# Starting layer one with its first Strassen product instead of the router's projection, and running its seven products in another order

## The chip, the core and the metric

The kernel runs on one core of a Trainium2 chip. A core has a matrix engine (TensorE, PE in the profile, with its weight loads shown apart as PEld), a vector engine (VectorE, DVE), a scalar engine (ScalarE, ACT), GpSimd (POOL), and SyncE (SP), which here issues nearly all transfers. Each engine takes its own instructions strictly in the order in which they were written down; engines meet only at semaphores. The metric is the time of one execution on the device in microseconds (us); lower is better.

## The reference, cut to what matters

Two layers run one after the other, each adding to `x` (8 sequences of 256 tokens, 1024 channels, float32 throughout).

```python
# layer one: dense weight W plus a mixture of 8 rank-16 adapters, 2 of 8 chosen per token
base   = einsum('btd,od->bto', x, W)
logits = einsum('btd,ed->bte', x, Wr) + one_hot(language_ids) * 5.0
topw, topi = top_k(logits, 2);  weights = softmax(topw)
gates  = sum(one_hot(topi) * weights)               # 8 per token
h      = einsum('btd,erd->bter', x, A)              # 8 x 16 per token
x = x + base + 2.0 * einsum('bter,bte,eor->bto', h, gates, B)
# layer two: one whole 1024 x 1024 weight per sequence, chosen by adapter id
x = x + einsum('bsi,boi->bso', x, weight[adapter_ids])
```

`language_ids` and `adapter_ids` are two lists of eight integers.

## The kernel before, in words

**Blocks.** In layer one `x`, `W` and the result are cut into 2 x 2 blocks (`xb`, `yb`, `wb`, keys "11", "12", "21", "22"; the first digit of an `xb` key is the half of the channels, the second the half of the tokens). With the identity added to the diagonal blocks of `W` (`add_identity`), `x + base` is one matrix product, and it is done with seven block products instead of eight (Strassen-Winograd). Inside each of the seven, `product` does the same once more: seven inner products on quarter blocks, so that a block product is seven groups of four 128x512 matmuls. It accumulates in PSUM banks named `A`, `B` and `X`, and its four result quarters are copied out by ScalarE (`evict` without a base) or added up by VectorE (`evict` with one). The sums and differences that an inner product takes as operands (`s1`, `t1`, `s2`, `t2`, `s3`, `t3`) are made by VectorE in `make_subs`; `late` makes two more in the middle of a product. Block-level sums come from `x_sum` and `w_sum`.

**Router.** `project(j, c)` multiplies a quarter of the tokens (half `j`, half of that `c`, 512 tokens) with `Wr` and all `A` together (136 columns, `aw_sb`, kept in block `y12` until that is needed): 32 matmuls over eight blocks `k` of 128 channels. VectorE then adds the language bias to the logits (`lg`), and ScalarE copies the adapter part out (`hT`). `gating(j)` is a chain of some twenty small VectorE operations (with one exponential on ScalarE in it) that finds the two largest logits and their weights, and ends with `onto_h`, which scales `hT` by the gates. `turn(j)` transposes `hT` on TensorE (`ps_g`) and copies it to `hg`. Four of the seven block products (2, 5, 3 and 4) take the adapters' part along: they get `lora` and `tokens`, and `mm` then adds two matmuls with `hg` to a group. The language ids reach all partitions through a small matmul with ones (`use_ids`); `use_adapter_ids` makes the adapter ids that layer two's loads read.

**Order.** From `manual_schedule` on, every engine's order is the order of the calls. VectorE's spare work is put in a list, `todo`, with a cost in us and a first place at which it may run; `pump(place)` after each inner product takes its share off that list. TensorE goes through: ten matmuls on the identity that only warm it up (`WARM`), `project(0, 0)`, `project(0, 1)`, `project(1, 0)`, `project(1, 1)`, `turn(0)`, and then the products 1 (with `turn(1)` behind it), 2, 5, 3, 6, 7, 4, and layer two's eight sequences (`adapt`).

**Transfers.** All 1-MB loads of `x` and `W` are issued by SP in the order of need; the first three pieces for the router's weights `awT` and the two lists of ids are issued by ScalarE. Eight completion semaphores go round, so a load waits until the load eight places earlier has landed. Layer two's weights (`load_w1`) overwrite blocks of `x` and `W` that are no longer needed, so each of these loads waits for the last reader of its block.

Of the kernel before, what the change touches and what calls it, by code (L numbers as in the profile page):

```python
# [16 lines left out]
P = 128  # L17
# [4 lines left out]
WARM = 10  # L22
# [3 lines left out]
def kernel(  # L26
# [25 lines left out]
    nc = tc.nc  # L52
# [30 lines left out]
    def flat(blk):  # L83
        return blk.rearrange("p k n -> p (k n)")

    def bank(name):
        return psum.tile([P, 2, TQ], F32, name=name, tag="acc")
# [8 lines left out]


    aw_sb = flat(yb["12"])[:, : KC * EA].rearrange("p (k e) -> p k e", k=KC)
    hT = [flat(yb["22"])[:, j * C * ER : (j + 1) * C * ER].rearrange("p (c e) -> p c e", c=C) for j in range(2)]
    b_sb = const.tile([ER, O], F32, name="b_sb")  # L100
    ids = const.tile([1, 2, NB], I32, name="ids")

    def load_x(queue, i, j, c, k0, k1):
        queue.dma_start(  # L104
            xb[f"{i+1}{j+1}"][:, k0:k1, c * TQ : (c + 1) * TQ], xT[i, j, c, :, k0:k1, :]
        )

    def load_w(i, j):
        nc.sync.dma_start(wb[f"{i+1}{j+1}"], wT[i, j])

    def load_aw(queue, k0, k1):
        queue.dma_start(aw_sb[:, k0:k1, :], awT[:, k0:k1, :])

    load_aw(nc.scalar, 0, 1)
    load_x(nc.sync, 0, 0, 0, 0, 1)
    load_aw(nc.scalar, 1, 3)
    load_x(nc.sync, 0, 0, 0, 1, 2)
    load_aw(nc.scalar, 3, 8)
    load_x(nc.sync, 0, 0, 0, 2, 4)
    load_x(nc.sync, 1, 0, 0, 0, 2)  # L120
    load_x(nc.sync, 1, 0, 0, 2, 4)
    load_x(nc.sync, 0, 0, 1, 0, 4)
    nc.scalar.dma_start(ids[:, 0, :], lang)
    nc.scalar.dma_start(ids[:, 1, :], adapt)
    load_x(nc.sync, 1, 0, 1, 0, 4)
    load_x(nc.sync, 0, 1, 0, 0, 4)
    load_x(nc.sync, 1, 1, 0, 0, 4)
    load_w(0, 0)
    load_x(nc.sync, 0, 1, 1, 0, 4)
    load_x(nc.sync, 1, 1, 1, 0, 4)  # L130
    nc.sync.dma_start(b_sb, bT)
# [12 lines left out]
    nc.vector.tensor_copy(desc, desc_i)  # L144
    ecol = const.tile([P, E], F32, name="ecol")
    nc.vector.tensor_copy(ecol, ecol_i)
    ids_f = const.tile([1, 2 * NB], F32, name="ids_f")
    bias = const.tile([P, NB, E], F32, name="bias")
    aid_i = const.tile([1, NB], I32, name="aid_i")
    ones = const.tile([1, P], F32, name="ones")  # L150
    nc.vector.memset(ones, 1.0)

    def use_ids():
        nc.vector.tensor_copy(ids_f, ids.rearrange("o t b -> o (t b)"))
        wide = bank("ids_wide")[:, 0, :NB]
        nc.tensor.matmul(wide, lhsT=ones, rhs=ids_f[:, :NB], start=True, stop=True)  # L156

        nc.vector.tensor_tensor(
            bias,
            wide.unsqueeze(2).to_broadcast([P, NB, E]),  # L160
            ecol.unsqueeze(1).to_broadcast([P, NB, E]),
            ALU.is_equal,
        )
        nc.vector.tensor_scalar(bias, bias, LANG_BIAS, None, ALU.mult)

    def use_adapter_ids():

        wrap = const.tile([1, NB], F32, name="wrap")
        nc.vector.tensor_scalar(wrap, ids_f[:, NB:], 0.0, float(NAD), ALU.is_lt, ALU.mult)
        nc.vector.tensor_tensor(wrap, ids_f[:, NB:], wrap, ALU.add)  # L170
        nc.vector.tensor_scalar(aid_i, wrap, 0.0, float(NAD - 1), ALU.max, ALU.min)
# [4 lines left out]
    def add(out_, x, y):  # L176
        tt(out_, x, y, ALU.add)
# [1 line left out]
    def minus(out_, x, y):  # L179
        tt(out_, x, y, ALU.subtract)  # L180

    def add_identity(blk):

        d = bass.AP(blk.tensor, blk.offset, [blk.ap[0], [OG + P, KH], [1, P]])
        add(d, d, ident.unsqueeze(1).to_broadcast([P, KH, P]))


    hg = [const.tile([ER, 2, TQ], F32, name=f"hg{j}") for j in range(2)]
    lg = [rpool.tile([P, C, E], F32, name=f"lg_{j}", tag=f"lg{j}") for j in range(2)]
    gate8 = {}  # L190

    def project(j, c):

        ps = bank(f"ps_h_{j}_{c}")
        for k in range(KC):
            for r in range(CQ):
                v, u = divmod(r, 2)
                nc.tensor.matmul(  # L198
                    ps[:, v, u * EA : (u + 1) * EA],
                    lhsT=xk(k, j, c)[:, ts(r, P)],  # L200
                    rhs=aw_sb[:, k, :],
                    start=(k == 0 and u == 0),
                    stop=(k == KC - 1),
                    skip_group_check=True,
                )
        if (j, c) == (0, 0):
            use_ids()
        ps = ps[:, :, : 2 * EA].rearrange("p v (u e) -> p v u e", u=2)
        split = lambda t: t[:, c * CQ : (c + 1) * CQ, :].rearrange("p (v u) e -> p v u e", v=2)
        nb = CQ * P // S  # L210
        b0 = (2 * j + c) * nb
        add(
            split(lg[j]),
            ps[:, :, :, ER:],
            bias[:, b0 : b0 + nb, :].unsqueeze(2).to_broadcast([P, nb, CQ // nb, E]),
        )
        nc.scalar.copy(split(hT[j]), ps[:, :, :, :ER])
# [49 lines left out]
    def turn(j):  # L267

        ps_g = bank(f"ps_g_{j}")
        for n in range(C):  # L270
            nc.tensor.transpose(ps_g[:, n // CQ, ts(n % CQ, P)], hT[j][:, n, :], ident)  # L271
        nc.scalar.copy(hg[j], ps_g)
# [9 lines left out]
    def b_part(rows):  # L282

        x = (b_sb[:, :OG], b_sb[:, OG:], bdiff[:, :OG])[rows]
        return x[:, :OQ], x[:, OQ:], bdiff[:, OG + rows * OQ : OG + (rows + 1) * OQ]
# [27 lines left out]
    def x_sum(fn, out_, x, y):  # L313
        return pieces(fn, xb[out_], xb[x], xb[y], 4)

    def w_sum(fn, out_, x, y):
        return pieces(fn, wb[out_], wb[x], wb[y], 2)
# [43 lines left out]
        else:  # L361
            add(dest, acc, base)

    def product(key, base, dest, lora=None, tokens=None):

        a, b, t, late = subs.pop(key)
        up = dict(zip("01d", b_part(lora))) if lora is not None else None

        def mm(acc, lhs, rhs, first=False, rows=None, c=0):
            steps = [(lhs[:, k, ts(m, P)], rhs[:, k, :], m) for k in range(2) for m in range(2)]  # L370
            if up is not None and rows is not None:
                steps += [(up[rows][:, ts(m, P)], hg[tokens][:, c, :], m) for m in range(2)]
            for i, (l, r, m) in enumerate(steps):
                nc.tensor.matmul(  # L374
                    acc[:, m, :],
                    lhsT=l,
                    rhs=r,
                    start=(first and i < 2),
                    stop=(i >= len(steps) - 2),
                    skip_group_check=True,  # L380
                )

        old = [base[:, q] if base is not None else None for q in range(4)]
        A = bank(f"A_{key}")
        mm(A, a(0, 0), b(0, 0), True)
        evict(dest[:, 0], A, old[0])
        pump(1)
        B = bank(f"B_{key}")
        mm(B, t["s1"], t["t1"], True, "1", 1)
        evict(dest[:, 3], B, old[3])  # L390
        pump(2)
        mm(A, t["s2"], t["t2"])
        evict(dest[:, 1], A, old[1])
        pump(3)
        X = bank(f"X_{key}")
        mm(X, a(0, 1), b(1, 0), True, "0", 0)
        add(dest[:, 0], X, dest[:, 0])
        late()
        pump(4)
        mm(A, t["s3"], t["t3"])  # L400
        add(dest[:, 3], A, dest[:, 3])
        pump(5)
        mm(B, t["s2"], b(1, 1), False, "d", 1)
        add(dest[:, 1], B, dest[:, 1])
        pump(6)
        mm(A, a(1, 1), t["t2"], False, "1", 0)
        evict(dest[:, 2], A, old[2])
        pump(7)
# [124 lines left out]


    ctx.enter_context(tc.manual_schedule())

    idle = bank("idle")
    for i in range(WARM):
        nc.tensor.matmul(idle[:, 0, :P], lhsT=ident, rhs=ident, start=True, stop=True)
    project(0, 0)  # L540
    project(0, 1)
    use_adapter_ids()
    for t in gating(0):
        t[2]()
    project(1, 0)
    add_identity(wb["11"])
    for t in make_subs("1", "11", "11"):
        t[2]()
    project(1, 1)
    todo += gating(1)  # L550
    turn(0)
    b_differences()
    add_identity(wb["22"])
    for t in w_sum(add, "21", "21", "22"):
        t[2]()

    y11, y12, y21, y22 = (yq(ij) for ij in IJ)

    def join(y, x):
# [1 line left out]
        return [(1.22, p, lambda q=q: add(y[:, q], y[:, q], x[:, q])) for q, p in ((0, 4), (3, 5), (1, 6), (2, 7))]  # L561


    todo += x_sum(minus, "12", "12", "11")
    todo += make_subs("2", "12", "21")
    product("1", None, y21)
    turn(1)
    todo += w_sum(minus, "11", "21", "11")
    todo += make_subs("5", "21", "12")
    product("2", y21, y11, 0, 0)  # L570
    todo += w_sum(minus, "12", "12", "11")
    todo += make_subs("3", "12", "22")
    product("5", None, y22, 1, 1)
    todo += x_sum(minus, "12", "22", "12")
    todo += make_subs("6", "11", "12")
    todo += w_sum(minus, "21", "22", "11")
    todo += x_sum(minus, "11", "12", "11")
    product("3", y22, y12, 2, 1)
    load_w1(0, "12", "22", "11")
    todo += make_subs("7", "21", "11")  # L580
    todo += join(y12, y21)
    product("6", y21, y21)
    load_w1(0, "21")
    todo += x_sum(minus, "21", "21", "12")
    todo += make_subs("4", "22", "21")
    todo += join(y22, y21)
    product("7", y21, y21)
# [59 lines left out]
```

## Time and profile before

| | us |
|---|---|
| median of three runs | 433.17 (433.10 to 433.33) |
| the profiled execution, its time | 433.07 |
| its span in the profile | 431.3 |
| TensorE busy in it | 424.4 (98%) |
| VectorE busy | 270.5 (63%) |
| ScalarE busy | 32.5 (8%) |

The span is the stretch from the first to the last instruction that the profiler saw; the execution's own time is 1.8 us more. A group line of the profile gives line, engine, operation, what is written and read, how often, then the busy time and the mean duration of one. A timeline line gives the start, the length, the engine, the line and the operation, how many records were merged, and in brackets how long the engine had been idle before it and who ended that. A float32 matmul leaves two records. Line 174 of the kernel before is the helper `tt`, so most VectorE work bears that number, and what it does is told by the tile names.

### The profile page before, as it was taken

What the parts mean: (1) busy time and instruction counts of PE and PEld (TensorE: products, weight loads), DVE (VectorE), ACT (ScalarE), POOL (GpSimd) and SP (SyncE); (2) the same over time, 40 slices, a digit from 0 to 9 for tenths busy, and PEclk for the clock granted to TensorE, in tenths of its full rate; (3) what the DMA queues carried; (4) which work ended last, traced back from release to release, by engine and by line L of the source; (5) the groups of instructions that cost most, each with busy time, mean ns of one, the idle gap of its engine ahead of it and who ended that gap; (6) DMA issues with size and microseconds to landing.
All of it is one profiled execution on the core that took longest, in us unless ns stands there. A gap on an engine that the chain in (4) does not pass through costs nothing.

```text
span 431.3 us, 3166 instructions
## 1 busy us (share of the span) xinstructions
PE 424.4 (98%) x1198; PEld 207.2 (48%) x1198; DVE 270.5 (63%) x325; ACT 32.5 (8%) x49; POOL 0.9 (0%) x8
## 2 busy tenths in 40 slices
PE   6999999999999999999999999999999999999996
PEld 6997444444444444444444444444444444444442
DVE  0068695743538887999765775575756576665521
ACT  0112210002000000000000101010110101010110
POOL 0000000000000000000000000000000000000000
PEclk9999999999999999999999999999999999999999
DMA  7995000000002040150202266555738476550202
GB/s 250 390 406 226 0 2 0 0 0 0 2 0 97 14 180 2 52 206 35 97 2 97 97 238 217 216 207 201 286 125 304 157 259 226 198 195 0 97 0 98
DMA packets 12643, 55.81 MB, mean 129 GB/s; under 512 B 1108, under 2 KB 1620, under 8 KB 8020
## 3 DMA queue, kind: packets, MB, share of 16 engines
q1 hardware_dynamic: 12048, 54.92, 35.3%
q10 hardware_dynamic: 580, 0.69, 0.5%
q8 instruction: 9, 0.15, 0.1%
q14 instruction: 6, 0.05, 0.0%
HBM read 47.22 MB, written 8.39 MB: 129 GB/s over the span
## 4 chain that ended last, share of the span: by engine, by line
PE 97%; DMA 2%; SPq 0%; DVE 0%; ACT 0%; issue 0%
PE A L479 25%; PE A L374 24%; PE B L374 14%; PE B L479 13%; PE X L374 7%; PE ps_h L198 7%; PE X L479 6%; DMA x<-xT_dram 2%; PE ps_g L271 0%; SPq L104 0%; DVE z L530 0%; ACT z L529 0%; PE ids_wide L156 0%
## 5 line engine op out<-in xcount | busy, mean ns | idle before, releaser
L479 PE MATMUL B<-x,x 128*128 128x512 f32 x128 | 57.5, 592 | 0.0
L374 PE MATMUL A<-t,s 128*128 128x512 f32 x112 | 50.3, 592 | 0.0
L479 PE MATMUL A<-w,x 128*128 128x512 f32 x96 | 43.2, 592 | 0.0
L479 PE MATMUL A<-w,y 128*128 128x512 f32 x96 | 42.7, 592 | 0.0
L479 PEld LDWEIGHTS B<-x,x 128*128 128x128 f32 x128 | 24.3, 190 | 30.6 <-issue 30.6
L174 DVE TENSOR_TENSOR w<-w,w 128x1024 f32<-128x1024 f32 x24 | 29.1, 1223 | 15.4 <-PE A L479 15.3
L174 DVE TENSOR_TENSOR y<-A,y 128x1024 f32<-128x1024 f32 x22 | 26.9, 1223 | 17.1 <-PE A L374 17.1
L374 PEld LDWEIGHTS A<-t,s 128*128 128x128 f32 x112 | 21.3, 190 | 26.8 <-issue 26.8
L198 PE MATMUL ps_h<-y,x 128*128 128x136 f32 x256 | 30.7, 280 | 1.8 <-DMA y<-awT_dram 1.0
L360 ACT COPY z<-A 128x512 f32<-128x512 f32 x23 | 13.5, 586 | 246.8 <-PE A L479 246.8
L198 PEld LDWEIGHTS ps_h<-y,x 128*128 128x128 f32 x256 | 29.9, 190 | 2.3 <-DMA y<-awT_dram 1.2
L479 PEld LDWEIGHTS A<-w,x 128*128 128x128 f32 x96 | 18.2, 190 | 23.0 <-issue 23.0
L479 PEld LDWEIGHTS A<-w,y 128*128 128x128 f32 x96 | 18.2, 190 | 23.0 <-issue 23.0
L374 PE MATMUL A<-x,w 128*128 128x512 f32 x56 | 25.2, 592 | 0.0
L374 PE MATMUL X<-x,w 128*128 128x512 f32 x56 | 25.2, 592 | 0.0
L374 PE MATMUL B<-x,s 128*128 128x512 f32 x56 | 25.2, 592 | 0.0
L374 PE MATMUL A<-t,w 128*128 128x512 f32 x56 | 25.2, 592 | 0.0
L374 PE MATMUL B<-t,s 128*128 128x512 f32 x56 | 25.2, 592 | 0.0
L174 DVE TENSOR_TENSOR y<-B,y 128x1024 f32<-128x1024 f32 x12 | 14.7, 1224 | 16.3 <-PE B L374 16.3
L174 DVE TENSOR_TENSOR y<-X,y 128x1024 f32<-128x1024 f32 x7 | 8.6, 1226 | 18.0 <-PE X L374 18.0
L174 DVE TENSOR_TENSOR x<-x,x 128x1024 f32<-128x1024 f32 x16 | 18.9, 1218 | 0.0
L174 DVE TENSOR_TENSOR t<-x 128x1024 f32<-128x1024 f32 x14 | 17.1, 1220 | 0.0
(96 smaller groups left out, 378.2 us busy)
## 6 DMA issues: line engine op xcount, KB each, us to landing
x<-w_dram SPq DMA_DIRECT2D x24, 1024.0 KB, 4.8
w<-w_dram SPq DMA_DIRECT2D x8, 1024.0 KB, 4.7
out_dram<-z SPq DMA_DIRECT2D x15, 512.0 KB, 3.3
x<-xT_dram SPq DMA_DIRECT2D x6, 1024.0 KB, 11.2
w<-wT_dram SPq DMA_DIRECT2D x4, 1024.0 KB, 15.6
x<-xT_dram SPq DMA_DIRECT2D x3, 512.0 KB, 6.4
x<-xT_dram SPq DMA_DIRECT2D x2, 256.0 KB, 5.0
b_sb<-bT_dram SPq DMA_DIRECT2D x1, 512.0 KB, 14.8
```

What stands on the lines that cost most here:

```text
L174: nc.vector.tensor_tensor(out_, x, y, op)
L198: nc.tensor.matmul(ps[:, v, u * EA : (u + 1) * EA], lhsT=xk(k, j, c)[:, ts(r, P)], rhs=aw_sb[:, k, :], start=(k == 0 and u == 0), stop=(k ...
L360: nc.scalar.copy(dest, acc)
L374: nc.tensor.matmul(acc[:, m, :], lhsT=l, rhs=r, start=(first and i < 2), stop=(i >= len(steps) - 2), skip_group_check=True,)
L479: nc.tensor.matmul(accs[name], lhsT=lhs[:, k // 2, k % 2, :], rhs=rhs[:, k, :], start=(first and k == 0), stop=(k == KH - 1), skip_group_c ...
```

## The change

Layer one's first block product is taken out of `product` and written out in a new function `opening`, and the router's work is moved behind or into it. In detail:

- `opening` runs the warm-up, then the inner products in another order: `X` first, then `A`, then half of the first router quarter (`project(0, 0, 0, KH)`), `B`, `A`, the other half of that quarter, and the last three. `X` takes the place of the first one copied out, and `A` is added to it.
- `w11` comes in four pieces with 1-KB rows instead of one load: the three pieces of its left half (columns 0 to 255) from ScalarE's queue, the right half from SP. The pieces of `x11` are issued in the order of `opening`'s use; `awT` is now cut in two (one half from each queue), and the two lists of ids are issued by GpSimd.
- `add_identity` on `w11` is done in two halves; the ids are converted in `use_adapter_ids`, and the matmul with ones is there twice, into the second half of the bank `idle`.
- The quarters `project(1, 0)`, `project(1, 1)`, `project(0, 1)` follow, in this order, with `b_differences`, the identity of `w22` and the sum for `w21` between the first two. `x12 - x11` is done in place in eight pieces of 128x512 behind `project(1, 1)`, then come `gating(1)` and `make_subs` of product 5. `turn(1)` stands right behind `project(0, 1)`, and `gating(0)` goes into the list for product 5, `turn(0)` behind that product.
- The seven products run in the order 1, 5, 2, 6, 3, 7, 4; the block sums and layer two's first loads move accordingly.
- `hT` lies in block `y11` instead of `y22`.

The core of the diff:

```diff
+    load_w11(nc.scalar, 0, 2, 3)
+    load_x(nc.sync, 0, 0, 0, 2, 3)
+    load_w11(nc.scalar, 0, 3, 4)
+    load_x(nc.sync, 0, 0, 0, 3, 4)
+    load_w11(nc.scalar, 0, 0, 2)
+    load_x(nc.sync, 0, 0, 0, 0, 2)
+    load_aw(nc.scalar, 0, 4)
+    load_w11(nc.sync, 1, 0, 4)
+    load_x(nc.sync, 0, 0, 1, 0, 2)
+    load_x(nc.sync, 0, 0, 1, 2, 4)
+    load_aw(nc.sync, 4, 8)
+    load_x(nc.sync, 1, 0, 0, 0, 4)
...
+    nc.gpsimd.dma_start(ids[:, 0, :], lang)
+    nc.gpsimd.dma_start(ids[:, 1, :], adapt)
...
+    def opening(key, dest):
+        idle = bank("idle")
+        for i in range(WARM):
+            nc.tensor.matmul(idle[:, 0, :P], lhsT=ident, rhs=ident, start=True, stop=True)
+        mm = multiply()
+        sums_of = make_subs(key, "11", "11")
+        a, b, t, late = subs.pop(key)
+        X = bank(f"X_{key}")
+        mm(X, a(0, 1), b(1, 0), True)
+        evict(dest[:, 0], X)
+        add_identity(wb["11"], 0, 2)
+        A = bank(f"A_{key}")
+        mm(A, a(0, 0), b(0, 0), True)
+        project(0, 0, 0, KH)
+        use_adapter_ids()
+        add_identity(wb["11"], 2, 4)
+        for s in sums_of[:4]:
+            s[2]()
+        add(dest[:, 0], A, dest[:, 0])
+        nc.tensor.matmul(idle[:, 1, :NB], lhsT=ones, rhs=ids_f[:, :NB], start=True, stop=True)
+        use_ids(idle[:, 1, :NB])
+        B = bank(f"B_{key}")
+        mm(B, t["s1"], t["t1"], True)
+        evict(dest[:, 3], B)
+        for s in sums_of[4:]:
+            s[2]()
+        mm(A, t["s2"], t["t2"])
+        evict(dest[:, 1], A)
+        project(0, 0, KH, KC)
+        late()
+        mm(A, t["s3"], t["t3"])
...
-    project(0, 0)
-    project(0, 1)
-    use_adapter_ids()
-    for t in gating(0):
-        t[2]()
+    opening("1", y21)
     project(1, 0)
-    add_identity(wb["11"])
-    for t in make_subs("1", "11", "11"):
-        t[2]()
-    project(1, 1)
-    todo += gating(1)
-    turn(0)
     b_differences()
     add_identity(wb["22"])
     for t in w_sum(add, "21", "21", "22"):
         t[2]()
...
-    todo += x_sum(minus, "12", "12", "11")
-    todo += make_subs("2", "12", "21")
-    product("1", None, y21)
+    project(1, 1)
+    for c in range(2):
+        for k in range(KH):
+            minus(xk(k, 1, c), xk(k, 1, c), xk(k, 0, c))
+    for t in gating(1) + make_subs("5", "21", "12"):
+        t[2]()
+    project(0, 1)
     turn(1)
+    todo += gating(0)
     todo += w_sum(minus, "11", "21", "11")
-    todo += make_subs("5", "21", "12")
-    product("2", y21, y11, 0, 0)
+    todo += make_subs("2", "12", "21")
+    product("5", None, y22, 1, 1)
+    turn(0)
...
+    product("2", y21, y11, 0, 0)
...
+    product("6", y21, y21)
+    load_w1(0, "21")
...
     product("3", y22, y12, 2, 1)
     load_w1(0, "12", "22", "11")
...
     product("7", y21, y21)
```

More of the change, by code (lines that the diff above doesn't have):

```diff
@@ L98 @@
     aw_sb = flat(yb["12"])[:, : KC * EA].rearrange("p (k e) -> p k e", k=KC)
-    hT = [flat(yb["22"])[:, j * C * ER : (j + 1) * C * ER].rearrange("p (c e) -> p c e", c=C) for j in range(2)]
+    hT = [flat(yb["11"])[:, j * C * ER : (j + 1) * C * ER].rearrange("p (c e) -> p c e", c=C) for j in range(2)]
     b_sb = const.tile([ER, O], F32, name="b_sb")
@@ L109, in load_w, with load_w11 @@
         nc.sync.dma_start(wb[f"{i+1}{j+1}"], wT[i, j])
+    def load_w11(queue, i, k0, k1):
+        cols = slice(i * OQ, (i + 1) * OQ)
+        queue.dma_start(wb["11"][:, k0:k1, cols], wT[0, 0, :, k0:k1, cols])
     def load_aw(queue, k0, k1):
         queue.dma_start(aw_sb[:, k0:k1, :], awT[:, k0:k1, :])
[L114 to L124, printed above, removed]
+    load_w11(nc.scalar, 0, 2, 3)
[10 more added lines that the diff above has]
+    load_x(nc.sync, 1, 0, 0, 0, 4)
     load_x(nc.sync, 1, 0, 1, 0, 4)
@@ L127 @@
     load_x(nc.sync, 1, 1, 0, 0, 4)
-    load_w(0, 0)
     load_x(nc.sync, 0, 1, 1, 0, 4)
@@ L151, with use_ids @@
     nc.vector.memset(ones, 1.0)
-    def use_ids():
-        nc.vector.tensor_copy(ids_f, ids.rearrange("o t b -> o (t b)"))
-        wide = bank("ids_wide")[:, 0, :NB]
+    def use_ids(wide):
         nc.tensor.matmul(wide, lhsT=ones, rhs=ids_f[:, :NB], start=True, stop=True)
@@ L166, in use_adapter_ids @@
     def use_adapter_ids():
+        nc.vector.tensor_copy(ids_f, ids.rearrange("o t b -> o (t b)"))
         wrap = const.tile([1, NB], F32, name="wrap")
@@ L180, in minus, with add_identity @@
         tt(out_, x, y, ALU.subtract)
-    def add_identity(blk):
-        d = bass.AP(blk.tensor, blk.offset, [blk.ap[0], [OG + P, KH], [1, P]])
-        add(d, d, ident.unsqueeze(1).to_broadcast([P, KH, P]))
+    def add_identity(blk, k0=0, k1=KH):
+        d = bass.AP(blk.tensor, blk.offset + k0 * (OG + P), [blk.ap[0], [OG + P, k1 - k0], [1, P]])
+        add(d, d, ident.unsqueeze(1).to_broadcast([P, k1 - k0, P]))
     hg = [const.tile([ER, 2, TQ], F32, name=f"hg{j}") for j in range(2)]
@@ L190, with project @@
     gate8 = {}
-    def project(j, c):
-        ps = bank(f"ps_h_{j}_{c}")
-        for k in range(KC):
+    projected = {}
+    def project(j, c, k0=0, k1=KC):
+        if k0 == 0:
+            projected[j, c] = bank(f"ps_h_{j}_{c}")
+        ps = projected[j, c]
+        for k in range(k0, k1):
             for r in range(CQ):
@@ L205, in project @@
                 )
-        if (j, c) == (0, 0):
-            use_ids()
+        if k1 < KC:
+            return
         ps = ps[:, :, : 2 * EA].rearrange("p v (u e) -> p v u e", u=2)
@@ L362, in evict, with multiply @@
             add(dest, acc, base)
-    def product(key, base, dest, lora=None, tokens=None):
-        a, b, t, late = subs.pop(key)
-        up = dict(zip("01d", b_part(lora))) if lora is not None else None
+    def multiply(up=None, tokens=None):
         def mm(acc, lhs, rhs, first=False, rows=None, c=0):
@@ L381, in mm, with product @@
                 )
+        return mm
+    def opening(key, dest):
[29 more added lines that the diff above has]
+        mm(A, t["s3"], t["t3"])
+        add(dest[:, 3], A, dest[:, 3])
+        mm(B, t["s2"], b(1, 1))
+        add(dest[:, 1], B, dest[:, 1])
+        mm(A, a(1, 1), t["t2"])
+        evict(dest[:, 2], A)
+    def product(key, base, dest, lora=None, tokens=None):
+        a, b, t, late = subs.pop(key)
+        mm = multiply(dict(zip("01d", b_part(lora))) if lora is not None else None, tokens)
         old = [base[:, q] if base is not None else None for q in range(4)]
@@ L535, with join @@
     ctx.enter_context(tc.manual_schedule())
-    idle = bank("idle")
-    for i in range(WARM):
-        nc.tensor.matmul(idle[:, 0, :P], lhsT=ident, rhs=ident, start=True, stop=True)
-    project(0, 0)
-    project(0, 1)
-    use_adapter_ids()
-    for t in gating(0):
-        t[2]()
-    project(1, 0)
-    add_identity(wb["11"])
-    for t in make_subs("1", "11", "11"):
-        t[2]()
-    project(1, 1)
-    todo += gating(1)
-    turn(0)
+    y11, y12, y21, y22 = (yq(ij) for ij in IJ)
+    def join(y, x):
+        return [(1.22, p, lambda q=q: add(y[:, q], y[:, q], x[:, q])) for q, p in ((0, 4), (3, 5), (1, 6), (2, 7))]
+    opening("1", y21)
+    project(1, 0)
     b_differences()
@@ L555 @@
         t[2]()
-    y11, y12, y21, y22 = (yq(ij) for ij in IJ)
-    def join(y, x):
-        return [(1.22, p, lambda q=q: add(y[:, q], y[:, q], x[:, q])) for q, p in ((0, 4), (3, 5), (1, 6), (2, 7))]
-    todo += x_sum(minus, "12", "12", "11")
-    todo += make_subs("2", "12", "21")
-    product("1", None, y21)
-    turn(1)
-    todo += w_sum(minus, "11", "21", "11")
-    todo += make_subs("5", "21", "12")
+    project(1, 1)
[5 more added lines that the diff above has]
+    project(0, 1)
+    turn(1)
+    todo += gating(0)
+    todo += w_sum(minus, "11", "21", "11")
+    todo += make_subs("2", "12", "21")
+    product("5", None, y22, 1, 1)
+    turn(0)
+    todo += x_sum(minus, "12", "22", "12")
+    todo += w_sum(minus, "21", "22", "11")
+    todo += make_subs("6", "11", "12")
+    t3 = x_sum(minus, "11", "12", "11")
+    todo += t3[:2]
     product("2", y21, y11, 0, 0)
@@ L572 @@
     todo += make_subs("3", "12", "22")
[L573 to L577, printed above, removed]
+    todo += t3[2:]
+    product("6", y21, y21)
+    load_w1(0, "21")
+    todo += make_subs("7", "21", "11")
+    todo += x_sum(minus, "21", "21", "12")
+    todo += join(y12, y21)
     product("3", y22, y12, 2, 1)
     load_w1(0, "12", "22", "11")
[L580 to L584, printed above, removed]
     todo += make_subs("4", "22", "21")
```

## The prediction

> **What bounds the kernel now.** First the page's shares and its chain.
>
> ```profile
> span 431.3 us, 3166 instructions
> PE 424.4 (98%) x1198; PEld 207.2 (48%) x1198; DVE 270.5 (63%) x325; ACT 32.5 (8%) x49; POOL 0.9 (0%) x8
> ...
> PE 97%; DMA 2%; SPq 0%; DVE 0%; ACT 0%; issue 0%
> ```
>
> TensorE is the bound, and the chain is its own work for 97%. So only two things can move the time: matmul work, which the change hardly touches, and the 431.3 - 424.4 = 6.9 us in which PE is not busy. The timeline of PE says where those lie.
>
> ```profile
> 1.41 3.93 PE L539 MATMUL idle<-ident 128*128 128x128 f32 x20 [1.41 <-POOL ident masks.py:199]
> 5.17 1.13 PE L198 MATMUL ps_h<-y,x 128*128 128x136 f32 x8
> 7.29 1.19 PE L198 MATMUL ps_h<-y,x 128*128 128x136 f32 x8 [0.98 <-DMA y<-awT_dram]
> 9.34 5.83 PE L198 MATMUL ps_h<-y,x 128*128 128x136 f32 x48 [0.86 <-DMA x<-xT_dram]
> 15.10 0.38 PE L156 MATMUL ids_wide<-ids_f,ones 1*128 1x8 f32 x2
> 15.41 22.51 PE L198 MATMUL ps_h<-y,x 128*128 128x136 f32 x192
> 37.76 1.04 PE L271 MATMUL ps_g<-ident,y 128*128 128x128 f32 x8
> 38.63 3.60 PE L374 MATMUL A<-x,w 128*128 128x512 f32 x8
> 42.06 3.60 PE L374 MATMUL B<-t,s 128*128 128x512 f32 x8
> ```
>
> The brackets: 1.41 before the first instruction, 0.98 and 0.86 for the router's first loads, then nothing more; the last matmul ends at 427.65, and 3.65 of tail makes up 6.9. **The change can win back 0.98 + 0.86 = 1.84 us at the most** (the first load lands no sooner than 5.1, see below), and PE has no other slack: every stall that it makes is paid in full. Prices from these starts: a group of eight records (four 128x512 matmuls) is 42.06 - 38.63 = 3.43; a router quarter of 64 records is 64/192 of 37.76 - 15.41 less the start of the transposes, 7.41 (the logits of successive quarters are picked up at 23.13, 30.54 and 37.96, which gives 7.41 too); the ones matmul is 15.41 - 15.10 = 0.31; eight transposes are 0.87.
>
> The price of VectorE's part comes from its own timeline (rows left out between the dots):
>
> ```profile
> 23.13 0.19 DVE L174 TENSOR_TENSOR lg<-ps_h,bias 128x32 f32<-128x32 f32 x1 [6.93 <-PE ps_h L198]
> 23.24 0.15 DVE L169 TENSOR_SCALAR wrap<-ids_f 1x8 f32<-1x8 f32 x1
> ...
> 23.69 0.20 DVE L227 TENSOR_REDUCE m<-lg 128x8 f32<-128x64 f32 x1
> ...
> 28.20 1.23 DVE L174 TENSOR_TENSOR y<-y,hot 128x1024 f32<-128x1024 f32 x1
> ...
> 31.37 0.69 DVE L174 TENSOR_TENSOR s<-w 128x512 f32<-128x512 f32 x1
> 31.98 1.22 DVE L174 TENSOR_TENSOR t<-x 128x1024 f32<-128x1024 f32 x1
> 33.11 0.68 DVE L174 TENSOR_TENSOR s<-s,w 128x512 f32<-128x512 f32 x1
> ```
>
> The first quarter-half that follows the ones matmul ends at 15.41 + 7.41 = 22.82, and its logits are taken at 23.13: 0.31 from PE to DVE. The next operation starts 0.11 later. A whole gating chain, from the first reduction to the end of `onto_h`, is 28.20 + 1.23 - 23.69 = 5.74. A 128x512 operation occupies VectorE for 31.98 - 31.37 = 0.61, a 128x1024 one for 1.13.
>
> **The change, part by part.** *The start.* ScalarE's first load is now 128 rows of `w11` in place of 128 rows of `awT` (whose issue at 0.74 landed at 5.07), SP's first is the same 256 KB of `x`; PE begins at 5.17 as before. Two matmuls (1.72) are then ready, to 6.89; the second pair is 128 rows of `w11` (128 KB) where before it was 128 rows of `awT` (136 KB), and the same 256 KB of `x`; that pair let PE start at 7.29. So a gap of 0.40, between 0 (they land with the first) and 0.98 (the old one). `X` ends at 9.01. `A` needs the third pair (256 KB of `w11` for 340 KB of `awT`, the same 512 KB of `x`), which before let PE start at 9.34, and for the `w11` piece one identity add of 256 columns on VectorE. The nearest row of that size (128x256 for `bdiff`, line 174) takes 0.42; the `w11` piece is the smaller of the pair, so I let the add run half beside the landing of `x`: `A` starts at about 9.56, a gap of 0.55, between 0.33 (9.34) and 1.0 (the whole add behind it, and hand-overs). Old gaps 1.84, new ones 0.95: **-0.89**.
>
> *The ids.* The ones matmul is issued twice: **+0.31**. Their loads go from ScalarE to GpSimd. No row here has such a load. Before, they were issued at 2.15 and 2.75 and read at 7.91; VectorE now stops for them ahead of the second identity add, `s1` and `t1`. PE reaches `B` at 9.56 + 3.43 + 3.71 + 0.62 = 17.3; the identity add, `s1` and `t1` are 0.42 + 0.69 + 1.22 and hand-overs, 2.5. So ids and loads may land as late as 14.8 for nothing, 13 us after GpSimd's last operation at 1.3. The same cover serves, on SP's queue, the right half of `w11` and the first half of the second quarter of `x11`: 2.8 MB up to there, at the 0.39 MB per us that the stretch from 10 to 37.7 shows (396 GB/s), and 1.6 MB landed by 9.3, is 12.5. I take nothing, and 0 to +2 as bounds. Further down that queue the bytes are the same as before; the last load was issued at 23.7 and took at most 17.4 to land, 41.1, and `w21` and `w22` are first read after `project(1, 0)`, at 45.6. The Trainium skill (DMA: Bandwidth & Descriptors, SWDGE vs HWDGE) calls loads issued by GpSimd slower at the start, with some 2 us fixed each; by that figure the ids would land near 5 as well, and the sum would stay.
>
> *Inside the opening.* `s2`, `t2`, `late` and the last three groups have 3.4 to 7 us of matmuls over each pair (0.69 + 1.22); `use_ids` stands behind them. The half quarter between hides the copying of `A` (1.01). Nothing.
>
> *The hand-over to product 5: the price of the change.* Opening and two quarters put the end T of `project(1, 1)` at 17.3 + 2 x 3.43 + 3.71 + 3 x 3.43 + 2 x 7.41 = 53.0. Count from T. PE goes on with `project(0, 1)` and reaches `turn(1)` at T + 7.41. What `turn(1)` reads comes out of `onto_h` of `gating(1)`, at the end of VectorE's queue: logits picked up at T + 0.31, next operation at + 0.11, eight 128x512 subtractions at 0.61 (4.88), gating 5.74, hand-over back 0.1: T + 11.14. **PE stalls for 11.14 - 7.41 = 3.73**, with nothing behind it that could go ahead. Bounds: 3.4 (no hand-over, each operation at the shortest spacing) and 4.8, since the second gating before took from 42.67 to 49.45, 6.78, when its exponential stood behind a copy on ScalarE. None of it is new work: before, `gating(0)` had the quarters (1, 0) and (1, 1) beside it, and `gating(1)` and the subtractions ran beside product 1, whose 24.0 us of matmuls hid them. That cover is what the new order takes away: at T only one quarter is left.
>
> After that, product 5's `B` needs `hg`: `s1` to `t3` (5.21), the logits of quarter (0, 1), two ScalarE copies (0.59 and 1.01) end 7.0 after `onto_h`; PE is there after 0.97 + 3.43 + 3.43 = 7.8. Covered by 0.8. `gating(0)` and `turn(0)` have all of product 5 (30.9) beside them.
>
> *The other order.* Same groups, same adapters. A product without adapters is 7 x 3.43 = 24.0 of matmuls, and VectorE has seven additions (7.9), `late` (1.8) and its list beside it. The fullest new ones are 6 (two sums of `w12`, two of `x11`, operands of 3: 19.5) and 7 (operands of 4, four joins: 19.5); the old product 7 held four sums more than the new one, 24.0, and PE never waited there. Nothing. Layer two's first loads: block 21 goes out after product 6, 12, 22 and 11 after product 3, with two products (24 and 31 us) before use, against a median of 4.8 from issue to landing. Nothing.
>
> Sum: -0.89 + 0.31 + 3.73 = **+3.15**. Against the profiled execution: 431.3 + 3.15 and the 1.77 around it, 436.2; it lies 0.1 under the median of the runs shown, within their spread.
>
> **A rule that speaks against it.** This trace's clock row at its end:
>
> ```profile
> 427.60:431.10 3.50, 0.04 (x1) 0.00 (x0) 0.42 (x1) 0.37 (x1) 0.00 (x0) 1.00 0.24 77
> 431.10:431.30 0.20, 0.00 (x0) 0.00 (x0) 0.00 (x0) 0.00 (x0) 0.00 (x0) 0.54 0.00 0
> ```
>
> The column before the last two is the granted clock: PE stopped at 427.65, and the clock held at 1.00 for 3.45 us and then fell. A stall of 3.73 is longer than that. The Trainium skill (TensorE: Matmul & The Clock Gate, Part 1) says why it need not fall: activity is counted in fixed windows of 3.4 us that do not start with the gap, and a whole one must be idle; by it the clock falls in (3.73 - 3.41)/3.41, one case in ten, and by its shorter advice (no gaps over 3 us) it falls always, which would add 1.7 for one window at half rate.
>
> **The rivals.** *The clock falls in the stall.* For it the row above; against it that the stall is barely longer than the one idle stretch after which it is seen to fall. Its price from rows: the warm-up took 3.0 us for 14 records before the clock rose, where nine took 0.8 afterwards, so a window of some 3 us at half the rate, 1.5, or two, 3: 437.7 to 439.2. *Late loads*: ids or `w11` pieces land after 14.8. Each us late is a us, and VectorE's stop passes it on: landing at 16 to 18 gives 437.4 to 439.4. For it: 1-KB rows, a queue not seen here; against it 13 us of cover. *The stall is hidden* (the other side): it goes if the chain behind T takes no more than 7.41; then -0.89 + 0.31 = -0.58, 432.6. It turns not slower from a chain of 8.0 on, so the subtractions would have to cost 1.7 together in place of 4.88, at 0.22 each, what a 128x64 operation costs here. Only if they ran ahead of the logits would that come near, and the call order puts them behind. Even with no gap left at the start the gain is 1.53.
>
> **Numbers.** Forecast 0.78 (all its bounds low 435.3, all high 438.3), clock 0.08, late loads 0.09, hidden stall 0.05. The time is the forecast's, 436.2. The range leaves out the hidden stall and the dear halves of the two other rivals: 435.3 to 438.0. About 0.2% (0.9 us) is what a measurement of this kernel can tell from no change: below 432.3 is faster, 0.02; 432.3 to 434.0 the same, 0.04 (the hidden stall, or half of it); slower 0.94.
>
> **What would show it.** PE idle just before `ps_g`, once, for 3.4 to 4.8 us, ended by VectorE's `y<-y,hot`; gaps near 7 and 9 us of together 0.3 to 1.6; no other idle of PE over 0.2 up to the tail; eight `x<-x,x` 128x512 rows between the logits and the reductions. It is wrong if `ps_g` does not wait, if `B` in the opening waits for `s1`, or if the clock column drops after the stall.

## The result: slower by 1.2%, and the times spread

| | us |
|---|---|
| before, six runs | 433.13 (433.10 to 433.51) |
| changed, six runs | 438.75 (437.01 to 440.03) |
| ratio | 1.0121, 95% interval 1.0095 to 1.0147 |
| profiled execution, its span | 437.4 (before 431.3) |

The sign of the forecast is right and its size is not: 436.2 was predicted, with 435.3 to 438.0 as the range. The runs fall into groups. Each run has a mean granted clock of TensorE over its span: two runs at 1.000 took 437.01 and 437.03; three at 0.995 and 0.996 took 438.55, 438.94 and 439.19; one at 0.990 took 440.03. The kernel before had 1.00 in its profile and spread over 0.4 us.

Of the changed kernel's page, the span, the engines' shares and the chain that ended last:

```profile
span 437.4 us, 3176 instructions
PE 427.2 (98%) x1200; PEld 208.5 (48%) x1200; DVE 271.8 (62%) x330; ACT 32.3 (7%) x49; POOL 2.0 (0%) x10
...
PE 94%; DVE 2%; DMA 2%; ACTq 0%; issue 0%; ACT 0%; DVEq 0%
```

TensorE is still the bound, but VectorE now has 2% of the chain, some 10 us. TensorE's timeline (start, length, engine, line, operation; in brackets the idle time before it and who ended that) shows where:

```profile
1.41 4.63 PE L398 MATMUL idle<-ident 128*128 128x128 f32 x20 [1.41 <-POOL ident masks.py:199]
5.83 1.96 PE L382 MATMUL X<-x,w 128*128 128x512 f32 x4
8.58 1.98 PE L382 MATMUL X<-x,w 128*128 128x512 f32 x4 [0.79 <-DMA w<-wT_dram]
11.45 3.70 PE L382 MATMUL A<-x,w 128*128 128x512 f32 x8 [0.88 <-DVE w L180]
...
40.30 22.40 PE L208 MATMUL ps_h<-y,x 128*128 128x136 f32 x192
66.14 1.06 PE L281 MATMUL ps_g<-ident,y 128*128 128x128 f32 x8 [3.44 <-DVE y L180]
67.04 5.29 PE L382 MATMUL A<-x,w 128*128 128x512 f32 x8
72.17 3.60 PE L382 MATMUL B<-t,s 128*128 128x512 f32 x8
75.60 1.88 PE L382 MATMUL B<-hg,b_sb 128*128 128x512 f32 x4
```

Three things are to be read here. The opening has gaps of 0.79 and 0.88, and `A` starts at 11.45 where 9.56 was predicted. The transposes wait 3.44 us for VectorE's `y` (that is `onto_h`). And the group `A` behind them lasts from 67.04 to 72.17, 5.13 us for eight records that take 3.43 everywhere else.

The three make up the difference. The three router quarters end at 40.30 + 3 x 7.41 = 62.53. In the kernel before, the same work ended where the second transposes begin, less the 0.87 of the first transposes in it, 62.66 - 0.87 = 61.79:

```profile
62.66 1.04 PE L271 MATMUL ps_g<-ident,y 128*128 128x128 f32 x8
```

That is +0.74 for the opening. From 62.53 to 66.14 the stall: +3.6. The slow group: 5.13 - 3.43 = +1.70. Together 6.0 of the 6.1 by which the span grew; no other gap is in the trace.

What started `A` so late stands in the chain that ended with it (start, length, what):

```profile
1.67 9.19 DMA w<-wT_dram
...
10.96 0.43 DVE w L180
11.45 3.70 PE A L382 x8
```

The third piece of `w11` landed at 10.87, and the identity add and its hand-overs took the rest. The third piece of `x11` had landed at 10.36 and `X` was done: neither held `A` up.

VectorE's timeline over the stall:

```profile
55.32 0.19 DVE L180 TENSOR_TENSOR lg<-ps_h,bias 128x32 f32<-128x32 f32 x1 [2.62 <-PE ps_h L208]
55.43 4.90 DVE L180 TENSOR_TENSOR x<-x,x 128x512 f32<-128x512 f32 x8
60.24 0.21 DVE L237 TENSOR_REDUCE m<-lg 128x8 f32<-128x64 f32 x1
...
64.76 1.23 DVE L180 TENSOR_TENSOR y<-y,hot 128x1024 f32<-128x1024 f32 x1
```

VectorE sat idle for 2.62 us waiting for the logits, then did the eight subtractions (4.8 to the next start), and only then the gating, which ended at 65.99.

And the granted clock (the column before the last two), in stretches of 3.4 us, called windows below, that are laid so that two of their ends are those of the clock's own records; the first figure after the length is TensorE's busy time:

```profile
60.58:63.99 3.41, 2.12 (x19) 1.92 (x17) 2.76 (x14) 0.21 (x1) 0.00 (x0) 1.00 0.00 0
63.99:67.41 3.42, 1.27 (x9) 1.13 (x10) 3.32 (x8) 0.00 (x0) 0.00 (x0) 1.00 0.00 0
67.41:70.83 3.42, 3.42 (x5) 1.35 (x4) 3.42 (x5) 0.00 (x0) 0.00 (x0) 0.50 0.02 5
70.83:74.24 3.41, 3.41 (x9) 1.52 (x8) 3.01 (x14) 2.42 (x3) 0.00 (x0) 1.00 0.00 0
```

The clock fell to half at 67.4, when PE was already at work again, and came back one stretch later. The stretch before the fall was not idle: 1.27 of 3.42 were busy, 0.9 of it with transposes. (A trace has no clock record before the first rise, and the column reads 1.00 there. That the warm-up runs at half rate is seen in its records: 20 from 1.41 to 5.83 are 0.22 us each, where the 28 like them that fill has later, below, take 0.12.)

### The profile page after: what moved, and what is told of

The parts are those of the page before. It is cut to its first block, busy times and chain, and to the rows that moved or that the text cites. A ratio compares the mean times of both kernels' runs of the same rounds, so it can differ in the third digit from the quotient of the medians.

```text
span 437.4 us, 3176 instructions
## 1 busy us (share of the span) xinstructions
PE 427.2 (98%) x1200; PEld 208.5 (48%) x1200; DVE 271.8 (62%) x330; ACT 32.3 (7%) x49; POOL 2.0 (0%) x10
## 4 chain that ended last, share of the span: by engine, by line
PE 94%; DVE 2%; DMA 2%; ACTq 0%; issue 0%; ACT 0%; DVEq 0%
PE A L532 25%; PE A L382 24%; PE B L382 14%; PE B L532 13%; PE X L382 6%; PE X L532 6%; PE ps_h L208 5%; DMA w<-wT_dram 2%; DVE x L180 1%; PE ps_g L281 0%; DVE y L180 0%; DVE hot L180 0%; DVE place L180 0%; ACTq L113 0%; DVE first L240 0%
## 5 line engine op out<-in xcount | busy, mean ns | idle before, releaser
L180 DVE TENSOR_TENSOR y<-A,y 128x1024 f32<-128x1024 f32 x23 | 28.1, 1223 | 18.6 <-PE A L382 18.6
L382 PE MATMUL A<-x,w 128*128 128x512 f32 x56 | 27.0, 627 | 0.9 <-DVE w L180 0.9
L180 DVE TENSOR_TENSOR x<-x,x 128x1024 f32<-128x1024 f32 (+1 forms) x20 | 19.2, 1004 | 0.0
L382 PEld LDWEIGHTS A<-x,w 128*128 128x128 f32 x56 | 11.0, 200 | 14.8 <-issue 13.1
L382 PEld LDWEIGHTS X<-x,w 128*128 128x128 f32 x56 | 10.7, 194 | 14.1 <-issue 12.2
```

Of the source, the lines that this page charges most:

```text
L180: nc.vector.tensor_tensor(out_, x, y, op)
L382: nc.tensor.matmul(acc[:, m, :], lhsT=l, rhs=r, start=(first and i < 2), stop=(i >= len(steps) - 2), skip_group_check=True,)
```

## The experiments

### Does the stall make the clock fall? (fill, fill7)

```diff
-    def turn(j):
+    def turn(j, fill=0):
         ps_g = bank(f"ps_g_{j}")
+        for i in range(fill):
+            nc.tensor.matmul(ps_g[:, 0, :P], lhsT=ident, rhs=ident, start=True, stop=True)
...
-    turn(1)
+    turn(1, 14)
```

> The change plus 14 matmuls of 128 columns on the identity (3.1 us at full rate) ahead of the transposes of turn(1), into the bank that the transposes then overwrite; VectorE's chain is untouched, so the transposes can't start earlier. Theory (the idle stretch makes the clock fall): granted clock 1.00 in every run, the group A behind the transposes 3.4 us in place of 5.1, and every run near 437.0, as the changed kernel's two runs at clock 1.00. Rival (the clock falls for another reason, such as the transposes or its own rhythm): clock still below 1.00 in about four runs of six, times 437 to 440.

Measured: 437.39 (437.07 to 437.40, four runs), clock 0.999 to 1.000 in all. TensorE's timeline:

```profile
62.04 3.29 PE L281 MATMUL ps_g<-ident 128*128 128x128 f32 x28
65.64 1.06 PE L283 MATMUL ps_g<-ident,y 128*128 128x128 f32 x8 [0.31 <-DVE y L180]
66.54 3.60 PE L384 MATMUL A<-x,w 128*128 128x512 f32 x8
69.97 3.60 PE L384 MATMUL B<-t,s 128*128 128x512 f32 x8
```

The transposes start no sooner than VectorE lets them, the useless matmuls fill the stretch, and `A` is back at 69.97 - 66.54 = 3.43. So the 1.7 us and the spread came from the clock, and the clock's fall from the idle stretch. The kernel's time with the stall alone is 437.0 to 437.4.

fill7 is the same with `turn(1, 7)`.

> The changed kernel with 7 matmuls on the identity ahead of the transposes (1.6 us) in place of 14, so that some 1.8 us of idle are left in the stretch. Theory (a clock window with half its time idle is enough to fall, since the window that ended in the fall had 2.1 of 3.4 us idle in one trace and 2.3 in another): clock below 1.00 in a minority of the runs, 437.0 to 439. Rival (only a stretch longer than a window, 3.4, makes it fall): clock 1.00 and 437.0 to 437.4 in every run.

Measured: 437.15 (436.81 to 437.53, four runs), clock 0.999 to 1.000 in all, with 1.88 us of idle left before the transposes. The theory as put expected some falls; in four runs there was none. It doesn't follow that only a stretch longer than 3.4 us counts, as the rival had it: in the trace of ids_scalar, below, the clock fell when PE had been idle for 2.26 us. The traces of the runs narrow down where the limit lies, because matmuls also stop at the end of each kernel. Two windows, the one of fill7 over its stall and the last of lean (a run below) with matmuls in it:

```profile
63.81:67.23 3.42, 1.67 (x10) 1.32 (x11) 3.35 (x6) 0.00 (x0) 0.00 (x0) 1.00 0.00 0
425.76:429.17 3.41, 1.21 (x3) 0.19 (x1) 0.42 (x1) 0.37 (x1) 0.00 (x0) 1.00 0.43 158
```

After the first the clock held, though 1.75 us of it, just over half, were idle; after the second it fell, 2.2 us after PE had stopped. Over all the traces it fell after such windows with 0.79, 1.07, 1.15, 1.19, 1.21 and 1.27 us busy and held after 1.67, 1.71 (reorder), 1.87, 1.93 and more. The limit in these traces lies between 1.27 and 1.67 of 3.41, and where the windows lie decides how an idle stretch is split over two of them.

### Does the order in VectorE's queue make the stall? (reorder)

```diff
+    for k in range(KH):
+        minus(xk(k, 1, 0), xk(k, 1, 0), xk(k, 0, 0))
     project(1, 1)
-    for c in range(2):
-        for k in range(KH):
-            minus(xk(k, 1, c), xk(k, 1, c), xk(k, 0, c))
-    for t in gating(1) + make_subs("5", "21", "12"):
+    for t in gating(1):
+        t[2]()
+    for k in range(KH):
+        minus(xk(k, 1, 1), xk(k, 1, 1), xk(k, 0, 1))
+    for t in make_subs("5", "21", "12"):
         t[2]()
```

> The first four of the eight 128x512 subtractions ahead of the call of project(1, 1), the other four behind gating(1). Theory (the order in VectorE's queue makes the stall): onto_h ends 0.31 + 0.11 + 5.74 = 6.2 us after the end of project(1, 1), before PE needs it at 7.41; no wait at ps_g, clock 1.00, and 437.0 - 3.4 = 433.6. Rival (the transposes wait for something else, ScalarE's copies or the bank): the wait of 3.4 stays, 437 or more.

Measured: 433.95 (433.65 to 434.63, eleven runs), ratio to before 1.0021 (1.0012 to 1.0030), clock 0.999 to 1.000. TensorE's timeline has no wait at the transposes any more:

```profile
62.06 1.04 PE L281 MATMUL ps_g<-ident,y 128*128 128x128 f32 x8
62.93 3.60 PE L382 MATMUL A<-x,w 128*128 128x512 f32 x8
66.37 3.60 PE L382 MATMUL B<-t,s 128*128 128x512 f32 x8
70.12 1.98 PE L382 MATMUL B<-hg,b_sb 128*128 128x512 f32 x4 [0.16 <-ACT hg L282]
```

The same operations in another order take 437.0 to 433.95 at full clock and 438.75 to 433.95 in the medians. What is late next is `hg`, by 0.16 us of idle, the chain that the prediction had covered by 0.8 only. Its price is larger than the bracket: from the start of `B` to the next `A`, 71.95, are 5.58 us, where the kernel before needed 5.15:

```profile
66.97 3.60 PE L374 MATMUL B<-t,s 128*128 128x512 f32 x8
70.41 1.88 PE L374 MATMUL B<-hg,b_sb 128*128 128x512 f32 x4
72.12 3.60 PE L374 MATMUL A<-t,s 128*128 128x512 f32 x8
```

That is 0.43 of the 0.8 us that reorder takes over the kernel before. The opening, which this edit doesn't touch, has 0.27 in this trace (the transposes start at 62.06, against 61.79).

### Why do the opening's loads land late? (ids_scalar, both, rows)

Predicted were the landings of the router's loads in the kernel before, 5.1, 7.2 and 9.3 us. The changed kernel's second pair let PE start at 8.58, and its third had landed at 10.87.

```diff
     load_aw(nc.scalar, 0, 4)
+    nc.scalar.dma_start(ids[:, 0, :], lang)
+    nc.scalar.dma_start(ids[:, 1, :], adapt)
...
-    nc.gpsimd.dma_start(ids[:, 0, :], lang)
-    nc.gpsimd.dma_start(ids[:, 1, :], adapt)
```

> The two loads of ids go from GpSimd's queue back to ScalarE's, behind its four other loads. Theory (the loads issued by GpSimd slow the first weight and x loads, which land 0.4, 1.3 and 1.6 us later than in the kernel before): the three pairs land near 5.1, 7.3 and 9.5 again, A of the opening starts near 9.8 in place of 11.4, time 1.3 to 1.6 us less at equal clock (435.5 at clock 1.00). Rival (the rows of 1 KB, ScalarE's table load at 3.1, or the first loads' order are the cause): landings within 0.3 us of the changed kernel's, time as there.

Measured: 438.85 (437.03 to 440.08, four runs), as the changed kernel (at full clock 437.03 against 437.01 and 437.03). In its trace the second half of `X` starts at 8.72 and `A` at 11.26. GpSimd's loads are not the cause: a miss for the theory. In this trace ScalarE's table load, too, stood at 5.74 instead of 3.11, and the second pair was no sooner. This execution also shows the clock at its worst, two stretches at half rate:

```profile
61.36:64.77 3.41, 1.15 (x10) 0.95 (x9) 2.79 (x15) 0.21 (x1) 0.00 (x0) 1.00 0.00 0
64.77:68.19 3.42, 2.25 (x9) 2.10 (x10) 3.42 (x5) 0.00 (x0) 0.00 (x0) 0.50 0.00 0
68.19:71.60 3.41, 3.41 (x5) 1.35 (x4) 3.34 (x6) 0.46 (x1) 0.00 (x0) 0.50 0.02 5
71.60:75.00 3.40, 3.40 (x9) 1.52 (x8) 2.11 (x11) 2.05 (x3) 0.00 (x0) 1.00 0.00 0
```

It fell at 64.77 after a stretch with 1.15 busy, and a stretch with 2.25 busy did not bring it back; only a full one did.

The two edits together:

> reorder and ids_scalar together. If both theories hold: 433.6 - 1.4 = 432.2, below the kernel before; if only the order holds: 433.6; if neither: 437 to 440.

Measured: 433.93 (433.47 to 434.23, eleven runs), as reorder alone.

Then the rows. The kernel is reorder, but the pieces of `w11` come from arrays in which each piece is one contiguous block; only the layout of the inputs changes.

```diff
-        queue.dma_start(wb["11"][:, k0:k1, cols], wT[0, 0, :, k0:k1, cols])
+        queue.dma_start(wb["11"][:, k0:k1, cols], {(0, 2): wa, (0, 3): wc, (0, 0): wd, (1, 0): we}[i, k0])
...
+    w11 = arrays["wT"][0, 0]
+    arrays |= {"wa": w11[:, 2:3, :256], "wc": w11[:, 3:4, :256], "wd": w11[:, 0:2, :256], "we": w11[:, :, 256:]}
```

> reorder, with the four pieces of w11 read from DRAM arrays of their own in which a piece is one contiguous block (before, a piece was 1 KB or 2 x 1 KB out of every 8-KB row). Theory (the first loads are slow because they pick 1 KB out of 8-KB rows): pairs land near 5.1, 7.3 and 9.5 as the router's did, A of the opening starts at 10.0 or sooner in place of 11.0, and 433.95 - 1.0 = 433.0. Rival (all that the kernel asks for at once, or the clock's later rise, sets the start): landings of the second and third pair stay at 8.0 to 8.7 and 10.4, time within 0.3 of 433.95.

Measured: 432.66 (432.52 to 432.89, eleven runs), 1.29 less than reorder, ratio to before 0.9988 (0.9979 to 0.9997). Its opening:

```profile
5.60 3.60 PE L386 MATMUL X<-x,w 128*128 128x512 f32 x8
9.72 3.70 PE L386 MATMUL A<-x,w 128*128 128x512 f32 x8 [0.52 <-DVE w L184]
```

No gap is left within `X`, and `A` starts 1.25 sooner than in reorder's trace (10.97) and 1.73 sooner than in the changed kernel's. Now the transfers: the last column is GB/s, the one before it the busy share of the 16 DMA engines. First the changed kernel, then rows, both from 2 to 8 us:

```profile
2.00:4.00 2.00, 2.00 (x11) 2.00 (x11) 0.00 (x0) 0.89 (x1) 0.68 (x2) 1.00 0.78 129
4.00:6.00 2.00, 2.00 (x11) 2.00 (x11) 0.00 (x0) 0.39 (x1) 0.00 (x0) 1.00 0.94 216
6.00:8.00 2.00, 1.79 (x5) 0.48 (x3) 0.00 (x0) 0.00 (x0) 0.00 (x0) 1.00 1.00 327
```

```profile
2.00:4.00 2.00, 2.00 (x11) 2.00 (x11) 0.00 (x0) 1.02 (x1) 0.68 (x2) 1.00 0.82 181
4.00:6.00 2.00, 2.00 (x11) 1.79 (x11) 0.00 (x0) 0.26 (x1) 0.00 (x0) 1.00 1.01 346
6.00:8.00 2.00, 2.00 (x6) 0.95 (x5) 0.00 (x0) 0.00 (x0) 0.00 (x0) 1.00 1.08 386
```

The DMA engines are about as busy in both, but move 216 against 346 GB/s from 4 to 6 us (reorder, whose opening is the changed kernel's, 219). Taking 1 KB out of every 8-KB row made the first loads slow.

### Trimming the start further (lean, lean_x)

lean is rows with `WARM = 8` and without the first of the two matmuls with ones.

> rows, with eight warm-up matmuls in place of ten and one matmul with ones in place of two. Theory (the cold warm-up holds X back, which in the profile started at 5.83 although its first loads had landed at 5.4, and the second ones matmul is 0.25 to 0.3 on the path): 0.25 + 0.4 less than rows. Rival (fewer warm-up matmuls let the clock rise later or the second pair is the bound anyway): only the 0.3 of the ones matmul, or nothing.

Measured: 432.45 (432.22 to 432.63, eleven runs), ratio to before 0.9981 (0.9972 to 0.9990): 0.2 less than rows, which is the ones matmul or less. In its trace `X` starts at 5.25 instead of 5.60, but the clock rose at 5.9 and `X` took 4.01. Nor is `X` what `A` waits for: PE idles for 0.55 until VectorE's identity add behind the third piece of `w11`, and `A` starts at 9.82 (in rows 9.72). A shorter warm-up has nothing to win in that trace. lean_x also reads the three first pieces of `x11` from contiguous arrays.

> lean, with the three first pieces of x11 too (2 KB or 4 KB out of 8-KB rows) read from contiguous arrays. Theory (picking part of a row slows the first loads, whichever matrix it is): the pairs land up to 0.5 us sooner, A of the opening starts at 9.3 to 9.6 in place of 9.8, time 432.0 to 432.3. Rival (only the 1-KB pieces of w11 were slow): 432.4 to 432.5, landings as in lean.

Measured: 432.21 (431.67 to 433.44, twelve runs), ratio to before 0.9980 (0.9971 to 0.9989): its interval and lean's nearly coincide. In its trace `X` starts at 4.99, but the third piece of `x11` landed at 9.85 in place of 8.20, and `A` waited 1.20 for it. The spread is the widest of all runs at full clock; inconclusive.

### The same in the kernel before (before_rows, before_rows_w6)

If rows were what held up the new opening, the old one should have had the same trouble: its two gaps stood behind pieces of `awT` and `x11`.

```diff
-    load_aw(nc.scalar, 0, 1)
-    load_x(nc.sync, 0, 0, 0, 0, 1)
+    nc.scalar.dma_start(aw_sb[:, 0:1, :], aa)
+    nc.sync.dma_start(xb["11"][:, 0:1, :TQ], xa)
...
+    aw, x11 = arrays["awT"], arrays["xT"][0, 0, 0]
+    arrays |= {"aa": aw[:, 0:1], "ac": aw[:, 1:3], "ad": aw[:, 3:8]}
+    arrays |= {"xa": x11[:, 0:1], "xc": x11[:, 1:2], "xd": x11[:, 2:4]}
```

> The kernel before, with its first six loads (three pieces of awT, 544 B to 2.7 KB out of 4.3-KB rows, and three of x11, 2 or 4 KB out of 8-KB rows) read from contiguous arrays. Theory (picking part of a row slows the first loads, whichever matrix): its two gaps of 0.98 and 0.86 shrink, and the time falls by 0.3 to 1.0 from 433.14. Rival (the router's start was not held up by this): gaps and time within 0.2.

Measured: 432.07 (431.81 to 432.41, eleven runs), ratio to before 0.9978 (0.9969 to 0.9987). TensorE's timeline, and the transfers from 2 to 6 us:

```profile
1.41 4.59 PE L545 MATMUL idle<-ident 128*128 128x128 f32 x20 [1.41 <-POOL ident masks.py:199]
5.83 8.15 PE L204 MATMUL ps_h<-y,x 128*128 128x136 f32 x64
```

```profile
2.00:4.00 2.00, 2.00 (x11) 2.00 (x11) 0.00 (x0) 0.00 (x0) 0.00 (x0) 1.00 0.92 303
4.00:6.00 2.00, 2.00 (x12) 2.00 (x12) 0.00 (x0) 0.00 (x0) 0.00 (x0) 1.00 0.97 355
```

303 GB/s from the second microsecond on (162 in the kernel before), and the two gaps, 0.98 and 0.86, are gone: the very gaps that the change set out to close, closed without any new order. Now the warm-up holds the start (the first loads had landed at 4.1). With `WARM = 6`:

> before_rows with six warm-up matmuls in place of ten; in its profile the router's first loads had landed at 4.1 while the ten cold warm-up matmuls held PE until 5.8. Theory (the warm-up is now what holds the start): PE's first real matmul near 4.15, some of the first work at half rate, 0.4 to 0.9 less than before_rows: 431.2 to 431.7. Rival (half-rate work gives it all back, or the clock rises later): 432.0 to 432.3.

Measured: 431.87 (431.64 to 432.25, eight runs), ratio to before 0.9971 (0.9960 to 0.9981). 0.2 less than before_rows, within its spread, and between the two forecasts, so it decides for neither. In the profiled execution (432.24, the slow end of the runs) PE's first real matmul starts at 4.18, but the first 16 records take 3.66 where they need 1.85 at full rate: there half-rate work gave it all back. It has the lowest median of this study; its interval overlaps that of before_rows.

## Why the prediction was wrong, step by step

**Sum of the predicted terms +3.15; measured in the profiled execution +6.1.** Two steps failed, the landings of the first loads and the chance that the clock falls. By its own steps:

- *What bounds the kernel*, that every stall is paid in full, and that the start has little to win: right.
- *The start, -0.89, and the ids, +0.31*: wrong in sign. Together -0.58 was predicted and +0.74 measured. The step that failed is the landing of the second and third pair. It went by piece sizes (128 KB for 136, 256 for 340), and took the rows of the kernel before as the price for the same bytes; but the new pieces pick 1 KB out of 8-KB rows. `A` started at 11.45 instead of 9.56, 1.89 late. Of that, 1.25 is the rows (10.97 in reorder, 9.72 in rows), and 0.48 is this execution (11.45 here; the same opening starts `A` at 10.97, 10.95 and 10.87 in the traces of reorder, fill and fill7). What is left, 0.16, goes with the identity add: it was let run half beside the landing of `x`, but the piece of `w11` landed last (10.87 against 10.36), so all of the add stood behind it. The warm-up, which ended at 5.83 and not at 5.17, since the clock rose at 5.98 (before at 4.45), held up `X` but not `A`. The doubled ones matmul cost 19.32 - 18.78 - 0.31 = 0.23.
- *Old gaps 1.84*: too small. From start to start, 16 records took 9.34 - 5.17 = 4.17 us where they need 16 x 7.41 / 64 = 1.85, so the old gaps cost 2.3. By the prediction's own path (`B` at 17.3, T at 53.0) the three quarters end at 60.4, which is 1.4 sooner than 61.79 and not the 0.58 of its sum. `B` started at 19.32 and T was 55.1: counted along the path, the opening missed by 2.1.
- *Ids by GpSimd, nothing*: right in the price, and the rival of late loads did not come about: the ids were converted at 11.4, with cover to 14.8, and `B` did not wait. But they landed at 9.4 and 10.2 and not near 5, where the prediction's figure of 2 us put them; the cover carried the step.
- *The hand-over to product 5, 3.73*: right, 3.6 (3.44 of idle), at its place and by its cause; reorder takes it away and leaves 0.43 at `hg`.
- *`hg` covered by 0.8; the new order of the products, nothing*: right; no other gap in the trace.
- *The clock falls in the stall*, a rival with 0.08: this is the step that threw the time out of the range. It happened in four runs of six. Its price was right (1.5 said, 1.70 measured, about 3 in the run at 0.990). Its chance was wrong, because it was taken from a rule: that a whole counting window of 3.4 us must be idle, one case in ten for a stretch of 3.73. The Trainium skill (TensorE: Matmul & The Clock Gate, Part 1) describes such windows, and the stretch of 3.4 us at half rate agrees with it; but the trace shows a fall after a window with 1.27 of 3.42 busy, and another with 1.15 of 3.41. A window is enough that is mostly idle. With 1.27 busy, that is 2.14 idle, taken as enough, and the place of the windows left to chance, a stretch of 3.44 leaves such a window in (1.27 + 1.30) / 3.41, three cases of four (an estimate from these traces); seen were four of six runs, and three of four in ids_scalar. The page's shorter advice (no gaps over 3 us, among its closing rules) came nearer here.

The opening's error of 1.3 and the clock's 1.7, less 0.1 for the stall, are the 2.9 between +3.15 and +6.1. At full clock the changed kernel takes 437.0, inside the predicted range, though the opening's term had the wrong sign: the range was wide enough, not the step right.

## What to carry to other kernels

When work is moved ahead on the bounding engine, look for the chain of another engine that loses its cover: here the same VectorE operations, in the same number, cost 3.6 us when the gating stood behind all eight subtractions, and 0.4 when four of them had moved ahead of the logits, into idle time, and four behind the gating. An idle stretch of 3.4 us on TensorE cost 1.5 to 3 us more than itself in seven of ten runs and made the times spread, so price such a stretch with the clock's fall included. And before a new order is built around a wait for first loads, look at how they read memory: contiguous pieces removed the same gaps in the old order.

## What the runs showed of the hardware beyond that

- The granted clock fell after windows of 3.41 us in which TensorE was busy for 1.27 us or less (six with some work in them, 0.79 to 1.27), and held after those with 1.67 or more. The 1.67 of fill7 hold 0.9 of transposes; without them they would be 0.77, far less than the 1.21, all of other matmuls, after which it fell in lean. By this one window, transposes count as work for the clock.
- The clock rose after windows with 3.04 us busy (the kernel before, 1.04 to 4.45 us) and more, and did not after 2.25 (ids_scalar) or 2.56 (before_rows_w6, 0.55 to 3.96 us).
- In the first microseconds the speed of the transfers went with how their rows lie: from 2 to 4 us 129 GB/s (1 KB and 2 KB out of 8-KB rows), 181 (only `x` and `awT` so), 303 (all contiguous). From 8 to 10 us the changed kernel's loads, pieces of rows still among them, ran at 382, so the slowness showed only at the start; what makes it so was not tried.
- Two tiny loads issued by GpSimd at 1.5 and 2.2 us landed at 9.4 and 10.2 in the changed kernel, with no other load in their queue.
